# Two graph layers on one core: the score row turned and sent before the first half of the row sums is added up and the second half is fetched

## The chip, the cores and the metric

The kernel runs on one core of a Trainium2 chip. The metric is the time of one execution in microseconds of device time. The kernel before takes 2389.66 us (median of 3 runs, 2389.35 to 2391.8).

The engines are called by the names of the profile: PE is the matrix engine (PEld its weight loads), DVE the vector engine, ACT the scalar engine, POOL the third elementwise engine, SP the engine that here issues nearly every DMA. Each engine works through its own instructions in order; between engines there are semaphores.

## The reference

The input is x (64 samples, 256 nodes, 512 features, float32) and a 256x256 adjacency matrix that all samples share. Two layers follow, each `x = x + layer(relu(layernorm(x)))`.

- Layer 0 is a graph attention with one head: `h = X W` (512 to 256 features), `e[i,j] = leaky_relu(h_i a0 + h_j a1)`, masked by the adjacency, softmax over j, `out = alpha h`, and the result is `[out, h]`, 512 wide again.
- Layer 1 is an attention with 8 heads of 64: q, k, v and the output have 512x512 weights with biases, the scores are masked by the same adjacency, softmax over the keys, and the output projection.

All products are in float32.

## The kernel before, in words

Two samples make a *group* (GB = 2, 512 rows); there are 32 groups (NG). The main loop takes the groups in turn, and each group in two *steps*, one for each sample (b = 0 and b = 1). A step holds the attention heads of layer 1 for sample (g, b), and, threaded between them, pieces of other work: the q, k, v projections of group g+1 (`project`), layer 0 of group g+2 (`first_layer`), the layer norm of the group g+3 (`first_norm`), the output projection of the sample before (`outputs`), and the row sums of this sample's softmax (`fold`). The order is written out by hand: the two strings in `steps` (L1176), one for each step, and an own string for the very first step (L1184). Each letter advances one generator up to its next `yield`: u a product of `project`, s a piece of `first_layer`, o a product of `outputs`, n a piece of `first_norm`, m a mask, f a piece of `fold`. At the start of each step `weigh` of the sample before and then `scores` of the current one are written (the letter S).

The 512x512 products and the first layer's product with W are done by a scheme of seven half-size products (Strassen's, Winograd's form) with sums formed on the elementwise engines. PE's instructions are chained one behind the other in the order in which they are written (`in_order`). On the other engines `not_sooner` ties one instruction behind the engine's last one; where it is not used, the tile framework's scheduler may move an instruction among its neighbours of the same engine.

What the change touches:

- `fold(g, b, p)` (L984): the sums of the masked exponentials. `put` writes a quad of four heads (512 KB) to DRAM ("rows"); `fetch` reads it back in another layout with four DMAs of 128 KB each ("parts", from SP); `add` sums the parts with two instructions on POOL; `sum_up` (L1013) turns a 128x256 block with a DVE transpose and reduces it on DVE into `compact`. The six f's of a step are: put 0 and fetch 0; put 1; add 0; **sum_up 0 and fetch 1**; add 1; sum_up 1 and the reciprocal. The parts of step b = 0 lie in the pool tag "e" with a single buffer, so that fetch 1 may only be issued when sum_up 0 has read the buffer.
- `score_rows(g)` (L621), called in `first_products` (L692) right after the sixth of the seven products of layer 0 is added into H: the layer's attention needs the score of every node along a row. DVE turns eight columns of H (128x32, "rows" from H), SP writes them to DRAM ("line", 2 KB), waits for that to land, and reads the line back broadcast to all 128 partitions ("own", 256 KB).
- `first_layer` (L699) then takes `own`: ACT adds the score of the other node for four blocks (`e<-own,H`), DVE applies the leaky relu (`e<-e`, L758 on), ACT the exponential, DVE the mask, and PE multiplies with H (`po`). The tile e (L748) has the same tag "e" with one buffer, so that ACT's first `e<-own,H` waits for `own` to land **and** for sum_up 1 of the current step to have read the parts.
- `weigh(g, b, p)` (L1038): DVE spreads `compact` into r, PE makes the products `pr`, DVE multiplies both (`oT<-pr,r`), which frees the PSUM banks of pr.
- `scores(g, b)` (L933): PE makes eight score blocks `sc` in four pairs; ACT takes each with an exponential (`p<-sc`), which frees its PSUM bank. In the built program the third pair goes into the banks that `p<-sc` of the first block and `oT<-pr,r` of the first quad set free, and waits for both.

So in the stretch around the change, fetch 1 and the score row's two DMAs stand behind each other on SP, sum_up 0 and the turn of the score row on DVE.

Of the kernel before, what the change touches and what calls it, by code (L numbers as in the profile page):

```python
# [57 lines left out]
def bounded(  # L58
# [24 lines left out]
    vector, scalar, gpsimd, sync = (  # L83
        Remembers(e) for e in (nc.vector, nc.scalar, nc.gpsimd, nc.sync)
    )
# [29 lines left out]
    def after(instruction, name):  # L115

        tc.add_manual_dep(
            instruction.ins, name,
            mybir.DependencyInfo(mybir.DependencyClass.NoSync, mybir.DependencyReason.DATA),
            reason="the engine's order",  # L120
        )

    def not_sooner(engine, operation, *args, **kwargs):

        last = engine.last
        after(getattr(engine, operation)(*args, **kwargs), last)
# [140 lines left out]
        not_sooner(gpsimd, "tensor_sub", t2, w22, w12)  # L267
        not_sooner(gpsimd, "tensor_sub", t4, w21, t2)

    put_last, norm_last, edge_last, sums_last, turn_last, fold_last = [], [], [], [], [], []  # L270

    def last_bias():

# [342 lines left out]
    H = const.tile([P, GT, F1 + 3], F32, name="H")  # L616
# [3 lines left out]

    def score_rows(g):  # L621
        rows = small.tile([P, GT, 8], F32, tag="rows", name=f"rows_{g}", bufs=2)
        last = vector.last
        turned = vector.transpose(rows.rearrange("p t c -> p (t c)"), H[:, :, 0:8])
        for other in [last, *fold_last] if g >= 2 else [last]:
            after(turned, other)
        line = dram.tile([P // 8, S], F32, tag="line", name=f"line_{g}")
        not_sooner(sync, "dma_start", line, rows.rearrange("p t c -> p (t c)")[::8, :])
        own = att.tile([P, P // S, GT, S], F32, tag="r", name=f"own_{g}", bufs=1)
        not_sooner(  # L630
            sync, "dma_start", own.rearrange("p k t j -> p (k t j)"),
            line.rearrange("(o k) j -> o (k j)", o=1).to_broadcast([P, TOK]),
        )
        return own.rearrange("p k t j -> p t k j")
# [209 lines left out]
    def project(g):  # L844
        ops = operands.pop(g)
        parts = {name: projection(g, name, ops) for name in "qkv"}
        for name in "qqkkqqqqqkkkkkvvvvvvv" if g == 0 else "q" * 7 + "k" * 7 + "v" * 7:
            next(parts[name])
            yield
# [78 lines left out]
    def value_differences(g, b):  # L928

        v = qkv["v", g, b][0]  # L930
        not_sooner(gpsimd, "tensor_sub", v[:, 1, :], v[:, 1, :], v[:, 0, :])

    def scores(g, b):  # L933

        (q, q_tag), (k, k_tag) = (qkv[name, g, b] for name in "qk")
        name = f"{g}_{b}"
        p = att.tile([P, NQ * QH, NT, N], F32, tag="p", name=f"p_{name}", bufs=1)
        for i in range(HP):  # L940
            sc = [f"sc_{name}_{2 * i + j}" for j in range(2)]
            sc = [held_bank(2, at) if at.endswith("_3") else mm(at) for at in sc]
            sc = [bank.rearrange("p (k n) -> p k n", k=NT) for bank in sc]
            for kb in range(NT):
                for j in range(2):
                    rows = slice(j * DH, (j + 1) * DH)
                    matmul(
                        sc[j][:, kb, :], k[rows, i, kb * P : (kb + 1) * P], q[rows, i, :],
                        start=True, stop=True,
                    )  # L950
            pair = p[:, 2 * i : 2 * i + 2]
            for j in range(2):
                last = scalar.last
                made = scalar.activation(pair[:, j], sc[j], AF.Exp, scale=scale)
                if g == b == 0:
                    others = [last, *put_last] if i > 1 else [last]
                else:
                    others = [last, *put_last, *norm_last, *edge_last]
                for other in others:
                    after(made, other)  # L960
        places.extend((q_tag, k_tag))
        return p
# [21 lines left out]
    def fold(g, b, p):  # L984

        if g == NG - 1:
            return
        compact = small.tile([P, NQ, N // S], F32, tag="compact", name=f"compact_{g}_{b}", bufs=2)  # L990
        row_sums[g, b] = compact
        pool, tag, bufs = (att, "e", 1) if b == 0 else (big, "hT0", 2)
        rows = []

        def put(quad):
            rows.append(dram.tile([P, QH, N], F32, tag="rows", name=f"rows_{g}_{b}_{quad}"))
            heads = slice(quad * QH, (quad + 1) * QH)
            not_sooner(sync, "dma_start", rows[quad], p[:, heads, 0, :])

        def fetch(quad):  # L1000
            parts = pool.tile([P, P // S, N], F32, tag=tag, name=f"parts_{g}_{b}_{quad}", bufs=bufs)
            for j in range(QH):
                not_sooner(
                    sync, "dma_start", parts[j * S : (j + 1) * S],
                    rows[quad][:, j, :].rearrange("(i a) n -> a i n", a=S),
                )
            return parts

        def add(parts):
            not_sooner(gpsimd, "tensor_add", parts[:, :2], parts[:, :2], parts[:, 2:])  # L1010
            not_sooner(gpsimd, "tensor_add", parts[:, 0], parts[:, 0], parts[:, 1])

        def sum_up(quad, parts):  # L1013
            not_sooner(vector, "transpose", parts[:, 1], parts[:, 0])
            vector.reduce_sum(
                compact[:, quad], parts[:, 1].rearrange("p (k a) -> p k a", a=S), axis=AX.X
            )
            fold_last[:] = [vector.last]

        put(0)  # L1020
        parts = fetch(0)
        yield
        put(1)
        yield
        add(parts)
        yield
        sum_up(0, parts)
        parts = fetch(1)
        yield
        add(parts)  # L1030
        yield
        sum_up(1, parts)
        vector.reciprocal(compact, compact)
        yield
# [138 lines left out]
    additions = (piece for g in range(NG) for piece in residual(g))  # L1173


    steps = ("Smmnfuuuumonmnuofuusssosfsfssuvnofunonfosuo", "Ssmmfusmusmfuososfuosfrsuuonufrounfouunsous")  # L1176
    waiting, late, folds = None, iter(()), iter(())
    for g in range(NG):
        products = project(g + 1) if g + 1 < NG else iter(())
        pieces = first_layer(g + 2) if g + 2 < NG else iter(())  # L1180
        for b, parts in enumerate(steps):
            if g == b == 0:

                parts = "Smmnfuuumnmnuufuussssfsfssuvnfrunnfsuu"  # L1184
            elif g == NG - 1:
                parts = "Smmoomoomooo"
            elif (g, b) == (NG - 2, 1):
                parts += "r"
            if waiting is not None:
                weigh(*waiting)  # L1190
                late = outputs(*waiting[:2])
            i, count = -1, sum(part not in "frv" for part in parts)
            for part in parts:
                i += part not in "frv"
                if part == "u":
                    next(products, None)
                elif part == "o":
                    next(late, None)
                elif part == "s":
                    next(pieces, None)  # L1200
                elif part == "n":
                    next(norms, None)
                elif part == "m":
                    next(masks)
                elif part == "f":
                    next(folds, None)
                    continue
                elif part == "r":
                    next(additions, None)
                    continue  # L1210
                elif part == "v":
                    if g < NG - 1:
                        value_differences(g, b)
                    continue
                else:
                    waiting = (g, b, scores(g, b))
                    masks = mask_pairs(waiting[2], g == NG - 1)
                    folds = fold(*waiting)
                if "v" not in parts and i == (count * 3 // 4, 6)[b] and g < NG - 1:
                    value_differences(g, b)  # L1220
                if i == count // 2:
                    if g == max(NG - 2, 0) and b == 1:
                        conclude()
                    if 0 < g < NG - 3:
                        load(g + 3, b)
                if b == 1 and i == 8 and g >= 2:
                    next(verdict, None)
        run(products)
        run(pieces)
# [373 lines left out]
```

## Time and profile before

| what | value |
|---|---|
| median of 3 runs | 2389.66 us (2389.35 to 2391.8) |
| the profiled execution's own time | 2390.06 us |
| its span in the trace | 2388.3 us |
| PE busy | 2375.2 us, 99% |
| DVE, POOL, ACT busy | 1705.2 us, 1430.5 us, 1023.0 us |
| DMA engines busy | 46.6% (all from SP's queue) |
| turn of the score row, DVE | 30 times, 0.20 us each |
| line, own (DMA) | 30 times, 2 KB and 256 KB |
| parts (DMA) | 496 times 128 KB, four to a fetch |

The page lists each engine's busy time, the chain of work that ended last, the costliest groups of instructions with the idle time before them, and the DMAs with the median time from issue to landing. The timeline lists the instructions of one engine in the order of time: start in us from the beginning of the span, duration, engine, line, operation, out<-in, shapes, and in brackets the idle time before it and what ended it. Nearly all rows say L35 or L137, the lines of the two helpers that record an instruction; so the rows are told apart by their tiles. Matmuls' ends are modelled by the profiler.

### The profile page before, as it was taken

What the parts mean: (1) busy time and instruction counts of PE and PEld (TensorE: products, weight loads), DVE (VectorE), ACT (ScalarE), POOL (GpSimd) and SP (SyncE); (2) the same over time, 40 slices, a digit from 0 to 9 for tenths busy, and PEclk for the clock granted to TensorE, in tenths of its full rate; (3) what the DMA queues carried; (4) which work ended last, traced back from release to release, by engine and by line L of the source; (5) the groups of instructions that cost most, each with busy time, mean ns of one, the idle gap of its engine ahead of it and who ended that gap; (6) DMA issues with size and microseconds to landing.
All of it is one profiled execution on the core that took longest, in us unless ns stands there. A gap on an engine that the chain in (4) does not pass through costs nothing.

```text
span 2388.3 us, 43029 instructions
## 1 busy us (share of the span) xinstructions
PE 2375.2 (99%) x15828; PEld 1993.8 (83%) x15828; DVE 1705.2 (71%) x3345; ACT 1023.0 (43%) x2017; POOL 1430.5 (60%) x1290
## 2 busy tenths in 40 slices
PE   9999999999999999999999999999999999999998
PEld 8888888888888888888888888888888888888886
DVE  7578676686766777767777667776677676777666
ACT  5444444343443444444444434444444444343431
POOL 4565655755657555666656575566665565655552
PEclk9999999999999999999999999999999999999999
DMA  5444445454445544454444455444554445554331
GB/s 185 129 147 146 145 130 163 149 151 143 140 143 155 168 144 137 133 163 149 146 146 140 152 150 161 150 135 139 163 151 146 143 134 161 151 161 141 107 109 46
DMA packets 271864, 343.49 MB, mean 144 GB/s; under 512 B 25376, under 2 KB 217120, under 8 KB 271648
## 3 DMA queue, kind: packets, MB, share of 16 engines
q1 hardware_dynamic: 271648, 340.69, 46.6%
q8 instruction: 126, 2.06, 0.4%
q14 instruction: 90, 0.74, 0.1%
HBM read 176.95 MB, written 163.64 MB: 143 GB/s over the span
## 4 chain that ended last, share of the span: by engine, by line
PE 95%; DVE 2%; ACT 1%; issue 1%; DMA 0%; POOL 0%; SPq 0%; DVEq 0%; ACTq 0%; POOLq 0%
PE pq L137 16%; PE pv L137 16%; PE py L137 16%; PE pk L137 15%; PE sc L137 10%; PE pr L137 9%; PE ph L137 8%; PE po L137 4%; DVE p L35 1%; DMA a_b<-in_L_gnn_a_dram 0%; ACT xn L35 0%; DVE x L35 0%; DVE st L35 0%; ACT e L35 0%; PE total L137 0%
## 5 line engine op out<-in xcount | busy, mean ns | idle before, releaser
L35 POOL TENSOR_TENSOR p<-p 128x512 f32<-128x512 f32 x248 | 393.0, 1598 | 480.9 <-DVE p L35 477.1
L35 ACT ACTIVATE xn<-x,factor 128x512 f32<-128x512 f32 x256 | 194.8, 807 | 412.2 <-POOL factor L35 405.0
L35 DVE TENSOR_TENSOR p<-p,maskT 128x1024 f32<-128x1024 f32 x254 | 347.4, 1389 | 3.2 <-ACT p L35 3.2
L35 DVE TENSOR_TENSOR x<-py,x 128x256 f32<-128x256 f32 x448 | 184.6, 412 | 204.1 <-PE py L137 197.9
L35 ACT ACTIVATE p<-sc 128x512 f32<-128x512 f32 x512 | 257.7, 627 | 94.7 <-PE sc L137 78.3
L35 POOL TENSOR_TENSOR parts<-parts 128x512 f32<-128x512 f32 x248 | 248.1, 1000 | 67.9 <-DMA parts<-rows 54.5
L137 PE MATMUL py<-wo_sb,oT 128*128 128x256 f32 x1024 | 262.4, 379 | 0.6 <-DVE oT L35 0.6
L137 PE MATMUL pk<-hT,wk_sb 128*128 128x256 f32 x1024 | 244.8, 382 | 0.0
L137 PE MATMUL sc<-q,k 64*128 64x256 f32 x2048 | 241.9, 385 | 0.1
L137 PE MATMUL pq<-hT,wq_sb 128*128 128x256 f32 x1024 | 240.1, 382 | 1.1 <-ACT hT L35 0.7
L137 PE MATMUL pv<-wv_sb,hT 128*128 128x256 f32 x1024 | 236.8, 379 | 0.0
L137 PE MATMUL pr<-p,v 128*32 128x256 f32 x4096 | 234.2, 380 | 0.0
L137 PEld LDWEIGHTS sc<-q,k 64*128 64x128 f32 x2048 | 190.8, 187 | 51.8 <-issue 26.3
L35 POOL TENSOR_TENSOR factor<-factor,rexp 128x2 f32<-128x2 f32 (+1 forms) x132 | 117.8, 892 | 178.7 <-DVE factor L35 178.2
L137 PEld LDWEIGHTS pq<-hT,wq_sb 128*128 128x128 f32 x1024 | 191.8, 190 | 36.7 <-issue 10.3
L137 PEld LDWEIGHTS py<-wo_sb,oT 128*128 128x128 f32 x1024 | 194.2, 190 | 28.2 <-DVE oT L35 1.1
L137 PEld LDWEIGHTS pk<-hT,wk_sb 128*128 128x128 f32 x1024 | 189.7, 190 | 33.3 <-issue 9.9
L137 PEld LDWEIGHTS pv<-wv_sb,hT 128*128 128x128 f32 x1024 | 194.6, 190 | 26.5
L137 PEld LDWEIGHTS pr<-p,v 128*32 128x32 f32 x4096 | 126.8, 110 | 97.8 <-issue 18.6
L137 PE MATMUL py<-wo_sb,o_sums 128*128 128x256 f32 x768 | 197.6, 380 | 0.5 <-DVE x L35 0.5
L137 PE MATMUL pv<-wv_sb,sums 128*128 128x256 f32 x768 | 184.2, 383 | 1.9 <-ACT kept_v L35 1.9
L137 PE MATMUL pq<-sums,wq_sb 128*128 128x256 f32 x768 | 181.5, 379 | 0.0
(150 smaller groups left out, 4066.3 us busy)
## 6 DMA issues: line engine op xcount, KB each, us to landing
passed<-xt SPq DMA_DIRECT2D x124, 512.0 KB, 2.9
moved<-passed SPq DMA_DIRECT2D x496, 128.0 KB, 3.5
rows<-p SPq DMA_DIRECT2D x124, 512.0 KB, 3.4
parts<-rows SPq DMA_DIRECT2D x496, 128.0 KB, 3.0
x<-in_x_dram SPq DMA_DIRECT2D x64, 512.0 KB, 4.5
out_dram<-x SPq DMA_DIRECT2D x62, 512.0 KB, 4.0
own<-line SPq DMA_DIRECT2D x30, 256.0 KB, 3.2
wq_sb<-in_L_gnn_Wq_dram SPq DMA_DIRECT2D x2, 512.0 KB, 9.6
```

The costliest lines, as they stand in the source:

```text
L35: instruction = getattr(self.engine, operation)(*args, **kwargs)
L137: in_order(nc.tensor.matmul(*args, **kwargs))
```

## The change

`score_rows` moves ahead of the fourth piece of `fold`. Three edits: in the string of step b = 0, and in that of the first step, the letters `fs` after the fifth s become `sf`, so that the sixth piece of layer 0 (product, sum into H, `score_rows`) is written before sum_up 0 and fetch 1; the list `fold_last`, which held the score row's transpose behind the sum of the row sums, goes; the transpose is tied behind DVE's last instruction alone.

```diff
-    put_last, norm_last, edge_last, sums_last, turn_last, fold_last = [], [], [], [], [], []
+    put_last, norm_last, edge_last, sums_last, turn_last = [], [], [], [], []
...
     def score_rows(g):
         rows = small.tile([P, GT, 8], F32, tag="rows", name=f"rows_{g}", bufs=2)
-        last = vector.last
-        turned = vector.transpose(rows.rearrange("p t c -> p (t c)"), H[:, :, 0:8])
-        for other in [last, *fold_last] if g >= 2 else [last]:
-            after(turned, other)
+        not_sooner(vector, "transpose", rows.rearrange("p t c -> p (t c)"), H[:, :, 0:8])
         line = dram.tile([P // 8, S], F32, tag="line", name=f"line_{g}")
...
         def sum_up(quad, parts):
...
-            fold_last[:] = [vector.last]
...
-    steps = ("Smmnfuuuumonmnuofuusssosfsfssuvnofunonfosuo", "Ssmmfusmusmfuososfuosfrsuuonufrounfouunsous")
+    steps = ("Smmnfuuuumonmnuofuusssosfssfsuvnofunonfosuo", "Ssmmfusmusmfuososfuosfrsuuonufrounfouunsous")
...
-                parts = "Smmnfuuumnmnuufuussssfsfssuvnfrunnfsuu"
+                parts = "Smmnfuuumnmnuufuussssfssfsuvnfrunnfsuu"
```

In the built program the orders of PE, ACT and POOL are the same as before. On SP, in 30 places (once in each group that still has a layer 0 to do), `parts` x4, `line`, `own` becomes `line`, `own`, `parts` x4. On DVE, in the same 30 places, the transpose of the score row goes from behind the transpose and the reduction of the row sums to ahead of them; in 29 of them the sum into H stood ahead of all three already, and in the first one it moves ahead as well. Two other DVE instructions change places with a neighbour, once each.

## The prediction

> **What bounds the kernel now.** I read the page first: engines' busy time and the chain that ended last.
>
> ```profile
> PE 2375.2 (99%) x15828; PEld 1993.8 (83%) x15828; DVE 1705.2 (71%) x3345; ACT 1023.0 (43%) x2017; POOL 1430.5 (60%) x1290
> PE 95%; DVE 2%; ACT 1%; issue 1%; DMA 0%; POOL 0%; SPq 0%; DVEq 0%; ACTq 0%; POOLq 0%
> ```
>
> PE is busy in all but 13 of 2388 us, and its order does not change. So there is little to win anywhere; what the change can do is make PE wait. 0.2% is 4.8 us, about what a measurement of this kernel can tell from no change. I therefore looked for the place where the moved work comes nearest to PE: the timelines of one typical group (around 1207 us; groups come 73.2 us apart and agree to a few hundredths), then the waits of the weight loads. SP and POOL:
>
> ```profile
> 1208.13 1.73 SPq L35 DMA_DIRECT2D parts<-rows  x4
> 1209.90 0.53 SPq L35 DMA_DIRECT2D line<-rows  x1
> 1212.86 0.34 SPq L35 DMA_DIRECT2D own<-line  x1
> 1215.23 0.34 SPq L35 DMA_DIRECT2D passed<-xt  x1
> ...
> 1212.87 2.08 POOL L35 TENSOR_TENSOR parts<-parts 128x512 f32<-128x512 f32 x2
> ```
>
> To be seen: SP stands still from the line's issue to its landing (own follows 0.07 us after it), and POOL adds the fetched parts when its factors are done, at 1212.87; the last part landed at 1212.62. DVE:
>
> ```profile
> 1206.83 0.43 DVE L35 TENSOR_TENSOR H<-ph,kept_h 128x258 f32<-128x258 f32 x1 [0.40 <-PE ph L137]
> 1207.17 0.44 DVE L35 STREAM_TRANSPOSE parts<-parts 128x256 f32<-128x256 f32 x1
> 1207.64 0.42 DVE L35 TENSOR_REDUCE compact<-parts 128x8 f32<-128x256 f32 x1
> 1207.98 0.20 DVE L35 STREAM_TRANSPOSE rows<-H 128x32 f32<-128x32 f32 x1
> ...
> 1216.38 0.42 DVE L35 TENSOR_TENSOR x<-py,x 128x256 f32<-128x256 f32 x1 [0.86 <-PE py L137]
> 1216.72 0.43 DVE L35 STREAM_TRANSPOSE parts<-parts 128x256 f32<-128x256 f32 x1
> 1217.19 0.42 DVE L35 TENSOR_REDUCE compact<-parts 128x8 f32<-128x256 f32 x1
> ...
> 1220.85 1.29 DVE L35 TENSOR_TENSOR oT<-pr,r 128x512 f32<-128x512 f32 x2
> ```
>
> The second parts' transpose does not wait for POOL (done at 1214.95) but for its turn behind `x<-py`. That is the cover of the whole change: 1.77 us. ACT and the weight loads:
>
> ```profile
> 1217.69 1.71 ACT L35 ACTIVATE e<-own,H 128x256 f32<-128x256 f32 x4 [1.28 <-DMA passed<-xt]
> 1221.02 4.03 ACT L35 ACTIVATE p<-sc 128x512 f32<-128x512 f32 x8 [0.24 <-PE sc L137]
> ...
> 1219.86 1.60 PEld L137 LDWEIGHTS sc<-q,k 64*128 64x128 f32 x16 [0.41 <-issue]
> 1221.67 1.60 PEld L137 LDWEIGHTS sc<-q,k 64*128 64x128 f32 x16 [0.22 <-ACT p L35]
> ```
>
> ACT's `e` starts 0.08 us after the reduction's end (1217.61): that frees the tile. The DMA named in brackets is not what it waited for; own had landed at 1216.1. And the loads for the third pair of score blocks already wait: for ACT's first `p<-sc` (ends 1221.62) and DVE's first `oT` (ends 1221.54). This is where the time of PE is decided.
>
> **The change, part by part.** Times are in this group, H's sum ending at 1207.26.
>
> *Turn of the score row first.* One DVE transpose of 0.20 us ahead of 0.86 us; it waits for H (0.03 us in the first group, where it stood right behind it). It ends at 1207.49, the line is issued 0.07 later, as parts were behind their reduction: 1207.56 instead of 1209.90. Sum_up 0 ends 0.3 later, hidden by DVE's idle 1.58 us before `x<-py` at 1210.33; without that cover it would cost its 0.3.
>
> *Own earlier.* Worth nothing: `e` waits for the reduction, and that stays.
>
> *Fetch 1 behind two DMAs and a landing.* What is new on SP ahead of the fetch: the line's landing x, 0.07, own's 0.34 and about 0.13 for the step to the next issue (0.05 between issues, four fulfilled waits of 17 ns). So it starts at 1207.56 + x + 0.54. The trace has no line alone: landing takes 2.5 at least, 2.8 in the median, but always 0.17 after the last part issued ahead of it. Above is thus 2.5; below is 1.7, the 128 KB stores of the output at the end (also SBUF to DRAM). I take 1.9, nearer to those, since the line's packets are done 1.7 to 2.0 after issue even behind the parts. Fetch: 1210.00, 1.87 late.
>
> *The landing of the fetch, T* (first issue to last landing). In these 30 groups 4.28 to 5.46, median 4.43, with only the 2 KB behind it. Now own's 256 KB go ahead and overlap it. Nearest row: the fetches of quad 0 issued behind a 512 KB load that lands about 1.6 us into them: 28 of them, median 4.69 (4.24 to 5.95). I take 4.8, bounds 4.3 and 5.45. Landed: 1214.80.
>
> *POOL's add:* 0.14 after the landing (0.12 to 0.16 where it waited), 2.08 long: 1214.94 to 1217.02. Nothing waits behind it on POOL, which idles 11.2 us afterwards.
>
> *DVE's second transpose:* 0.03 after POOL, 1217.05 instead of 1216.72: 0.33 late. Behind it on DVE stand the reduction, the leaky relu, r and `oT`; ACT's `e` waits for the reduction, and behind `e` on ACT stand the exponentials and all eight `p<-sc`.
>
> *PE:* ACT's path has 0.24 us in hand before `p<-sc`, DVE's only 0.08 (1221.62 less 1221.54). So PE waits s = 0.33 - 0.08 = 0.25 us more in front of the third pair. In general s = x + T - 6.45, and zero below. On SP nothing else is reached: `passed` waits for DVE until 1215.2, the fetch is issued by 1211.7.
>
> *The first group* differs:
>
> ```profile
> 108.10 1.06 PE L137 MATMUL ph<-w_more,hT 128*128 128x129 f32 x8
> ...
> 109.94 0.45 DVE L35 STREAM_TRANSPOSE parts<-parts 128x256 f32<-128x256 f32 x1 [1.14 <-POOL parts L35]
> ...
> 110.91 1.73 SPq L35 DMA_DIRECT2D parts<-rows  x4
> ...
> 117.95 0.40 DVE L35 STREAM_TRANSPOSE parts<-parts 128x256 f32<-128x256 f32 x1
> ```
>
> H's sum, moved ahead of that wait, ends at 109.16 + 0.42 = 109.58; line at 109.88, fetch at 112.32 instead of 110.91, landed 117.12, POOL 117.26 to 119.35, transpose 119.38: 1.43 late. ACT goes from `e` to `p<-sc` without idle time there, and PE's sc already takes 4.37 instead of 3.81 us, so I count 1.4 in full (0.7 to 2.7 with the bounds).
>
> *Sum:* 29 x 0.25 + 1.4 = 8.7 us on the profiled execution's 2390.06. That run is 0.4 above the median of the runs shown, so 2398.4.
>
> [...]
>
> **The rivals.**
>
> *The cover holds (not slower).* One mechanism: fetch 1 still lands in time. It decides at x + T = 6.45 (6.57 for 0.2%). For it: the line with nothing ahead of it may land in 1.7, and the fetch alone needs 4.4: together 6.1. Against it: own's 256 KB in the same DMA engines. Price: s = 0, the first group's 0.7 to 1.2 us alone: 2391, the same within 0.2%.
>
> *The late end (much slower).* x is 2.5 and the fetch, contending with own, takes 5.45: s = 1.5, 29 x 1.5 + 2.7 = 46 us, 2436. For it: landings of 5.3 to 5.5 occur in two groups, and 5.95 behind a load. Against it: medians are 4.4 and 4.7. Halfway (s = 0.9) is 2418.
>
> *A gain.* If the earlier own let `e` start sooner, the loads' present wait (0.22 us, of which PE loses 0.09 in its steps between matmuls) could go: 30 x 0.09 = 2.7 us, 2387, still within 0.2%. Against it: `e` starts behind the reduction, which stands behind `x<-py` as before.
>
> **How the numbers follow.** x + T is 6.7, the bounds 6.0 and 7.95. I give 0.66 to more than 6.57 (slower by over 0.2%; some 0.12 of it to the late end), 0.30 to the cover holding, 0.04 to the gain and anything else, 0.03 of which beyond 0.2%. So faster 0.03, same 0.31, slower 0.66. The likeliest case's own range is 2394 to 2412. The whole range goes from 2390 (cover holds, first group's least price) to 2420 (s = 0.95); the end at 2436 is left out.
>
> **What would show it.** In the changed kernel line is issued about 0.3 us after H's sum, own near 2.3, the first part near 2.7 (before 0.9), the last landing near 7.5 (5.4); POOL's add begins at that landing, not behind its factors; DVE's second transpose waits for POOL, by 0.3 us; the wait of sc's loads grows from 0.2 to near 0.5 us, and the groups come 73.4 instead of 73.2 us apart. Wrong would make it: a line landing below 1.6, a T untouched by own, or another consumer of the late DVE and ACT work that I took to be covered, such as the mask products behind `p<-sc`, 1 us ahead of PE's `po`.

## The result and the profile after

The changed kernel takes 2427.17 us (median of 5 runs, 2424.72 to 2428.97), the kernel before beside it 2389.66 us (5 runs, 2389.35 to 2391.8). The ratio is 1.0154, with an interval of 1.0139 to 1.0169: 37.5 us slower. The direction is the predicted one, the size is not: 8.7 us were predicted, and the end of the range was 2420. The profiled execution of the changed kernel took 2428.97 us, 38.9 more than the profiled one of before; what follows is read from it.

The page's busy times and its chain that ended last:

```profile
PE 2394.3 (99%) x15828; PEld 2011.0 (83%) x15828; DVE 1718.8 (71%) x3345; ACT 1020.3 (42%) x2017; POOL 1429.8 (59%) x1290
PE 78%; DMA 7%; DVE 4%; ACT 3%; POOL 3%; issue 3%; SPq 2%; POOLq 0%; DVEq 0%; ACTq 0%
```

PE is no longer nearly alone on the chain (78%, before 95%): DMA, POOL, DVE and ACT now have shares of it, so something that was covered has come out. PE's busy time grew by 19 us although it has the same instructions; some matmuls follow each other more slowly (in the group below sixteen take 2.26 us instead of 2.00), some run at a granted clock of 0.50 (6.83 us of the first group, 3.41 us of group 14).

A typical group, one 73 us period of the loop. The timelines of SP, POOL, DVE, ACT and the weight loads, with the start in us, the duration, the instructions, and in brackets the idle time before and what ended it:

```profile
1231.37 0.53 SPq L35 DMA_DIRECT2D line<-rows  x1
1233.13 0.35 SPq L35 DMA_DIRECT2D own<-line  x1
1233.78 1.73 SPq L35 DMA_DIRECT2D parts<-rows  x4
...
1239.19 2.08 POOL L35 TENSOR_TENSOR parts<-parts 128x512 f32<-128x512 f32 x2 [2.44 <-DMA parts<-rows]
```
```profile
1230.67 0.43 DVE L35 TENSOR_TENSOR H<-ph,kept_h 128x258 f32<-128x258 f32 x1 [0.40 <-PE ph L137]
1231.13 0.21 DVE L35 STREAM_TRANSPOSE rows<-H 128x32 f32<-128x32 f32 x1
...
1240.22 0.42 DVE L35 TENSOR_TENSOR x<-py,x 128x256 f32<-128x256 f32 x1 [0.86 <-PE py L137]
1241.31 0.45 DVE L35 STREAM_TRANSPOSE parts<-parts 128x256 f32<-128x256 f32 x1 [0.67 <-POOL parts L35]
```
```profile
1242.29 1.71 ACT L35 ACTIVATE e<-own,H 128x256 f32<-128x256 f32 x4 [2.04 <-issue]
...
1245.92 1.86 PEld L137 LDWEIGHTS sc<-q,k 64*128 64x128 f32 x16 [0.62 <-ACT p L35]
```

H's sum ends at 1231.10. The line is issued 0.27 later, lands in 1.69 (own follows 0.07 behind), and fetch 1 starts at 1233.78, 2.68 behind H's sum instead of 0.88. POOL's add begins 0.14 after the last part has landed, so the landing is at 1239.05 and the fetch took 5.27. POOL, which before went straight on from its factors, stands idle for 2.44 us. The second transpose on DVE is no longer in its turn behind `x<-py` (that would be 0.34 after 1240.22, at 1240.56) but waits for POOL: 0.75 late. At the end of this chain the weight loads for the third pair of score blocks wait 0.62 us (before 0.22) and then follow each other more slowly (1.86 for the sixteen instead of 1.60). PE's matmuls of the third and the fourth pair show the wait:

```profile
1245.92 2.26 PE L137 MATMUL sc<-q,k 64*128 64x256 f32 x16 [0.22 <-ACT p L35]
```

The group's 32 score matmuls take 3.81 us before and here 4.48 (2.00, a wait of 0.22, and 2.26): 0.67 lost, 0.08 less than the transpose's delay, as the prediction's formula has it.

Over the whole run, the waits (in total, how often, the longest) of the weight loads and of POOL, in the kernel before:

```profile
PEld sc L137 <- ACT p L35: 7.0, 31, 0.5
```
```profile
POOL parts L35 <- DMA parts<-rows: 54.5, 38, 5.2
```

And in the changed kernel:

```profile
PEld sc L137 <- ACT p L35: 32.7, 30, 3.0
```
```profile
POOL parts L35 <- DMA parts<-rows: 140.7, 63, 5.2
```

Taken from the traces group by group, with "lost" the time by which PE's way from the start of a group's scores to the start of the next group's is longer than before, groups 1 to 29 lost 34.9 us and the first group 4.9, together 39.8. The first group's scores start 0.4 sooner than before, so PE's last matmul comes 39.4 later. In groups 1 to 29 the second transpose is 1.15 late in the mean and the third pair of scores stalls 1.09. Two groups stand out. The first one:

```profile
112.23 1.73 SPq L35 DMA_DIRECT2D parts<-rows  x4
117.78 2.09 POOL L35 TENSOR_TENSOR parts<-parts 128x512 f32<-128x512 f32 x2 [3.73 <-DMA parts<-rows]
...
124.68 4.05 PE L137 MATMUL sc<-q,k 64*128 64x256 f32 x16 [2.58 <-ACT p L35]
128.66 3.12 PE L137 MATMUL pk<-sums,wk_sb 128*128 128x256 f32 x8
```

PE stands idle for 2.58 us, and then its work is slow: sixteen score matmuls take 4.05 us instead of 2.0, eight `pk` 3.12 instead of 1.99. The granted clock says why. In the windows of the trace the columns are the window, its length, the busy time (and instructions) of PE, PEld, DVE, ACT and POOL, the granted clock, the DMA share and GB/s:

```profile
120.74:124.15 3.41, 1.36 (x14) 0.87 (x10) 2.59 (x5) 2.95 (x7) 1.59 (x2) 1.00 0.00 0
124.15:127.56 3.41, 2.88 (x13) 2.88 (x15) 3.29 (x7) 2.71 (x6) 0.00 (x0) 0.50 0.02 5
127.56:130.98 3.42, 3.42 (x12) 2.32 (x10) 3.00 (x4) 1.40 (x3) 1.48 (x1) 0.50 0.00 0
```

For 6.8 us the clock is 0.50. The other is group 14 (near 1172 us), which lost 4.33: its line took 3.62 to land, PE was idle for 2.36 us, and one stretch of 3.4 us ran at 0.50. In the profile of before the clock is 0.5 only at the very end, from 2386.7 us on, when PE's last matmul is 4 us past.

### The profile page after: what moved, and what is told of

The parts are those of the page before. It is cut to its first block, busy times and chain, and to the rows that moved or that the text cites. A ratio compares the mean times of both kernels' runs of the same rounds, so it can differ in the third digit from the quotient of the medians.

```text
span 2427.3 us, 43032 instructions
## 1 busy us (share of the span) xinstructions
PE 2394.3 (99%) x15828; PEld 2011.0 (83%) x15828; DVE 1718.8 (71%) x3345; ACT 1020.3 (42%) x2017; POOL 1429.8 (59%) x1290
## 4 chain that ended last, share of the span: by engine, by line
PE 78%; DMA 7%; DVE 4%; ACT 3%; POOL 3%; issue 3%; SPq 2%; POOLq 0%; DVEq 0%; ACTq 0%
PE pq L137 16%; PE pv L137 16%; PE py L137 12%; PE pk L137 9%; PE sc L137 8%; PE ph L137 7%; PE pr L137 5%; DMA parts<-rows 5%; PE po L137 4%; POOL parts L35 2%; ACT e L35 2%; DMA line<-rows 2%; SPq L35 2%; DVE e L35 1%; DVE p L35 1%
## 5 line engine op out<-in xcount | busy, mean ns | idle before, releaser
L137 PE MATMUL sc<-q,k 64*128 64x256 f32 x2048 | 256.8, 389 | 20.7 <-ACT p L35 20.6
L137 PEld LDWEIGHTS sc<-q,k 64*128 64x128 f32 x2048 | 203.2, 188 | 74.2 <-ACT p L35 32.7
L137 PE MATMUL pk<-sums,wk_sb 128*128 128x256 f32 x768 | 182.7, 381 | 0.0
```

The source lines that it names most:

```text
L137: in_order(nc.tensor.matmul(*args, **kwargs))
```

## The experiments

Theory A: own's 256 KB, issued ahead of fetch 1, are still being moved when the fetch's parts are, and lengthen it; the rest of the loss is the later start. The rival, theory B: the late start alone is the cause, and where the fetch then falls among other work makes it long; own's bytes do not matter. The parts of the change were then done one at a time. The shorthand for all diffs: `score_rows` is cut into `turned_row` (DVE's turn), `sent_row` (line) and `spread_row` (own), without other changes; the diffs are against the changed kernel unless told otherwise.

**Line ahead of the fetch, own behind it.** SP then need not wait for the line's landing before the fetch, and own comes after the parts.

```diff
-        owns[g] = score_rows(g)
+        line = sent_row(g, turned_row(g))
         residual_from(1)
         yield
+        owns[g] = spread_row(g, line)
         product(first, 3, False)
```

> Score row turned and the line sent first, then sum_up 0 and the four DMAs of fetch 1, then own. The fetch no longer waits for the line's landing, and own's 256 KB stand behind it. Theory A (the loss comes from fetch 1 standing behind the line's landing and own, so that POOL's add, DVE's second transpose and ACT's e come late): the fetch starts near 1.1 us after H's sum (before 0.9, after 2.7), lands near 5.6, no group is late, 2390 us within 5. Rival C (the turn of the row ahead of sum_up 0 on DVE, or the line's DMA ahead of the fetch, costs by itself): stays near 2420 or more.

Measured: 2391.05 us, ratio 1.0003 (0.9994 to 1.0013). The fetch starts 1.21 after H's sum and takes 4.35 (median), the transpose is in its turn in every group from 1 to 29, and the wait of the weight loads is back at its old size:

```profile
PEld sc L137 <- ACT p L35: 7.2, 30, 0.9
```

So all but 1.5 of the 37.5 us hang on own, and the wait for the line that it brings, standing ahead of the fetch. The same kernel was run a second time, on another chip:

> The kernel of e1 (line, fetch 1, own) once more, beside the other runs of this call: 2390 to 2391 us, same as before.

Measured: 2391.41 us, 1.0005 (0.9995 to 1.0015), the same again. Its fetch took 4.55 in the median, where the first run's took 4.35: so differences of 0.2 between medians of T are within the spread.

**The wait alone, without own's bytes.** SP reads 64 bytes of the line into a tile that nobody uses, which makes it wait for the line's landing; then come fetch 1, and own behind it.

```diff
+        line = sent_row(g, turned_row(g))
+        probe = small.tile([1, 16], F32, tag="probe", name=f"probe_{g}", bufs=2)
+        not_sooner(sync, "dma_start", probe, line[0:1, :16])
         residual_from(1)
         yield
+        owns[g] = spread_row(g, line)
```

> Line sent first, then a DMA of 64 bytes that reads the line, so that SP waits for its landing as in the changed kernel, then fetch 1, and own last. The fetch starts as late as in the changed kernel (2.7 us after H's sum), but own's 256 KB stand behind it. Theory A (half of the loss is the wait, the other half is the fetch sharing the DMA engines with own ahead of it): first issue to last landing falls from 5.35 to about 4.5, s from about 1.1 to 0.25 in the mean (the late landings of the line keep some), first group near 1.5: 2399 us, 2394 to 2406. Rival B (the fetch takes longer because it runs later, beside other traffic, and not because of own): 5.3 stays, 2420 to 2427.

Measured: 2397.01 us, 1.0032 (1.002 to 1.0045). This is the run that separates the theories: its fetch starts 2.52 after H's sum in the median, nearly as late as in the changed kernel (2.69), but nothing of own is ahead of it. A group of it on SP, POOL and DVE, and the weight loads' wait over the run:

```profile
1283.75 0.53 SPq L35 DMA_DIRECT2D line<-rows  x1
1285.44 0.24 SPq L35 DMA_DIRECT2D probe<-line  x1
1285.97 1.74 SPq L35 DMA_DIRECT2D parts<-rows  x4
...
1290.49 2.08 POOL L35 TENSOR_TENSOR parts<-parts 128x512 f32<-128x512 f32 x2 [1.36 <-DMA parts<-rows]
```
```profile
1292.94 0.44 DVE L35 STREAM_TRANSPOSE parts<-parts 128x256 f32<-128x256 f32 x1
```
```profile
PEld sc L137 <- ACT p L35: 9.6, 32, 1.9
```

The fetch goes from 1285.97 to 1290.35 (POOL's start less 0.14): 4.38, and the median over the groups is 4.36, before 4.44. DVE's transpose has no wait in its brackets here: the cover of 1.77 us just holds. It does not in 11 of the 29 groups, six of them with a line that landed late and the others with a longer fetch; the mean delay is 0.13. The wait for the line costs 7.4 us in all, about 1.4 of it in the first group. The remaining 30 us come with own ahead of the fetch. A start 0.17 later (own's issue takes longer than the 64 bytes') is some 5 of them (29 x 0.17, an estimate from the medians); the rest is the longer fetch and what follows from it. Theory B falls.

**Half of own ahead.** own goes in two DMAs of 64 partitions (128 KB) each, one ahead of fetch 1 and one behind.

```diff
-        owns[g] = score_rows(g)
+        line, own = sent_row(g, turned_row(g))
+        spread_half(line, own, 0)
         residual_from(1)
         yield
+        spread_half(line, own, 1)
```

> The changed kernel with own in two DMAs of 64 partitions (128 KB): one ahead of fetch 1, the other behind it. If the fetch is lengthened by the bytes of own that go ahead of it (none: 4.35 us, 256 KB: 5.35, 256 + 128 KB: 6.5), it takes about 4.85 here; s falls from 1.1 to 0.6 in the mean: 2390 + 29 x 0.6 + 2 = 2409 us, 2404 to 2414. If the presence of a DMA ahead counts and not its bytes: 2422 or more.

Measured: 2415.11 us, 1.0103 (1.0086 to 1.012). The fetch takes 4.80 in the median, halfway between 4.35 and 5.34: what counts is how much goes ahead, and not that a DMA does. Half of the partitions is half of the bytes and half of the packets, so this run does not tell these two apart. The time is 6 us above what was expected; the first group stalls 2.30 and group 14, whose line took 3.63 to land, again falls into a stretch at half clock.

**More bytes ahead.** The changed kernel with a second DMA behind own, which spreads half of the line (128 KB) to a tile that nobody reads.

```diff
+        twin = small.tile([P, TOK // 2], F32, tag="twin", name=f"twin_{g}", bufs=1)
+        not_sooner(
+            sync, "dma_start", twin,
+            line[: P // 16].rearrange("(o k) j -> o (k j)", o=1).to_broadcast([P, TOK // 2]),
+        )
         return own.rearrange("p k t j -> p t k j")
```

> The changed kernel with a second DMA behind own and ahead of the fetch, which spreads half of the line once more over 128 partitions (128 KB, read by nobody). Theory A: the fetch starts 0.4 later (one more issue) and takes about 0.45 longer, so s grows by 0.85 in the mean: 29 x 0.85 on 2427 gives 2452 us, more where PE's idle time passes 2.3 us and its matmuls run at half rate behind it. Rival B (own's traffic does not matter, only the issue): 29 x 0.4, 2439 us.

Measured: 2492.71 us, 1.0436 (1.0418 to 1.0453), well above both. The fetch starts 0.43 later, as expected, but it takes 6.50, that is 1.16 longer than in the changed kernel and not 0.45, and the transpose is 2.74 late in the mean. So theory A has the direction and not the size: with 128 KB each, own's first half cost 0.45, its second 0.54 and the copy 1.16. The packets, the pieces in which the DMA engines move a transfer, fit better. In one group, counted from own's issue to the landing of the fetch in the changed kernel (1233.13 to 1239.04 us) and to shortly before it here (1261.1 to 1268.0):

```profile
DMA packets 721, 0.80 MB, mean 136 GB/s; under 512 B 80, under 2 KB 592, under 8 KB 720
```
```profile
DMA packets 879, 1.00 MB, mean 144 GB/s; under 512 B 96, under 2 KB 736, under 8 KB 877
```
own has 128 packets of 2 KB (720 less 592), so its half 64, and the fetch 512 of 1 KB (592 less 80). The copy of half the line comes in packets of 1 KB, and there are 128 of them (736 less 96, less the fetch's 512), as many as own has. By packets ahead the fetch is longer by 0.45 for 64, 0.99 for 128 and 2.15 for 256: nearly in proportion, which by bytes (128, 256, 384 KB) it is not. No run changed the size of the packets at equal bytes, and own, its half and the copy all read the same 2 KB of DRAM, so that it is the packets is argued and not shown.

Beyond the delay the clock sets in: 13 stretches at half clock within the run, a mean granted clock of 0.991.

**The turn alone.** DVE turns the score row early, as in the change; line and own stay where they were before.

```diff
-        owns[g] = score_rows(g)
+        rows = turned_row(g)
         residual_from(1)
         yield
+        owns[g] = spread_row(g, sent_row(g, rows))
```

> The turn of the score row ahead of sum_up 0 on DVE, as in the changed kernel; SP's order as before (fetch 1, line, own). Theory A: the DVE part is covered, 2390 us within 5. Rival C (DVE's order carries the loss): near 2427.

Measured: 2389.84 us, 1.0001 (0.9991 to 1.001). Sum_up 0 being 0.3 later is free, as predicted.

**The first group as before.** In the string of the very first step the letters are put back; all other groups stay changed.

```diff
-                parts = "Smmnfuuumnmnuufuussssfssfsuvnfrunnfsuu"
+                parts = "Smmnfuuumnmnuufuussssfsfssuvnfrunnfsuu"
```

> The changed kernel, with the letters of the very first step as before; the other 29 groups keep the change. Theory A: the first group's own price goes (4.9 us in the changed kernel's trace: 2.6 us of waiting and the half-rate matmuls behind it), 2427 to 2422.5. Rival (the first group costs as much as any other, near 1.2): 2426.

Measured: 2421.85 us, 1.0141 (1.0126 to 1.0157). The first group is worth 5.3 us (2427.17 less 2421.85) of the 37.5.

**A try at something better.** In the kernel before, sum_up 1 is written one piece sooner, so that `e` on ACT might start sooner and the weight loads' old wait shrink.

```diff
-    steps = ("Smmnfuuuumonmnuofuusssosfsfssuvnofunonfosuo", ...
+    steps = ("Smmnfuuuumonmnuofuusssosfsfssuvnofunofnosuo", ...
```

> The kernel before, with sum_up 1 one piece sooner in step b = 0, so that on DVE it stands ahead of the two transposes of xn and the last output sums. POOL's add is done at 7.7 us after H's sum, so the second transpose starts near 7.8 instead of 9.5, and ACT's e waits for own's landing (8.4 to 9.0) instead: 1 us sooner. If the small wait of the third pair's loads (0.2 us, of which PE loses 0.09) is all that this place costs, 29 x 0.09 = 2.6 us: 2387 us, within 0.2%. If the transposes of xn that come 0.9 us later delay the next norm, no gain or a loss.

Measured: 2392.72 us, 1.0014 (1.0004 to 1.0023), a miss. In the built program the transpose of the parts still stands behind `x<-py`, 9.47 after H's sum as before; only the two transposes of `xn` went behind it, which makes the leaky relu 0.34 later (11.72 instead of 11.38). On PE each group loses about 0.1, and the loads of `pv` wait 11.7 us in all for ACT, where they waited 9.3 before. No version beat the kernel before.

The series in one table (groups 1 to 29 of each profiled execution; start and T, from the first issue to the last landing, are medians, the other two are means; T of the wait-only kernel is worked out from POOL's start; the time is the median of the runs):

| kernel | fetch 1 after H's sum | sent ahead of it | T | transpose late | stall of scores | time, us |
|---|---|---|---|---|---|---|
| before | 0.88 | nothing | 4.44 | 0 | 0 | 2389.66 |
| line ahead, own behind | 1.21 | 2 KB | 4.35 | 0.00 | 0.02 | 2391.05 |
| wait alone | 2.52 | 2 KB, 64 B | 4.36 | 0.13 | 0.10 | 2397.01 |
| half of own ahead | 2.81 | 128 KB, 64 packets | 4.80 | 0.74 | 0.71 | 2415.11 |
| the change | 2.69 | 256 KB, 128 packets | 5.34 | 1.15 | 1.09 | 2427.17 |
| the change and a half | 3.12 | 384 KB, 256 packets | 6.50 | 2.74 | 3.12 | 2492.71 |

## Why the prediction was right in direction and wrong in size

*The mechanism* is the predicted one, link by link: the line goes out 0.27 behind H's sum, SP waits for its landing, fetch 1 lands late, POOL and then DVE's second transpose wait for it, and PE waits for the third pair of scores. The formula s = late - 0.08 holds in the groups where no stretch at half clock follows. The cover on DVE of 1.77 us is real too: the wait-only kernel uses it up and pays little. The mechanism was right, then, and sizes of its terms were not.

*The turn on DVE and the later sum_up 0, counted at nothing*: right (the turn alone, 1.0001).

*The line's landing x, taken as 1.9*: 1.91 in the mean, so the term fits, but as a mean of two cases: 1.67 to 1.72 in some twenty groups and 2.0 to 3.6 in the others. That the mean came out is partly luck: the rows it was taken from did not show these two cases.

*The landing of the fetch, T, taken as 4.8 with bounds of 4.3 and 5.45: the step that failed.* It measured 5.41 in the mean, at its upper bound in the middle of the groups and not now and then. My nearest row was a fetch behind a 512 KB load that lands 1.6 us into it. Here own is issued 0.65 ahead of the first part and takes 3.6 us to land (the page's median), so it lands 2.95 us into the fetch: the overlap is nearly twice as long as in the row I used. The experiments give the size: 0.45 for the first half of own ahead, 0.54 for the second. The packets in the trace show the overlap: in the median of the twenty groups with a line of 1.7, own's packets run until 2.45 us into the fetch, and the fetch's own end 4.49 after its first issue, where they end at 3.51 with own behind. So it is shown that own ahead makes T long, and that the two run at the same time; that the row I used was too short because of its shorter overlap is argued.

*The step on SP from own to the fetch, 0.34 + 0.13 = 0.47*: 0.66 measured in the mean (0.58 to 0.98), 0.2 more. In the typical group above it is 0.35 and then 0.30 to the first part's issue. In that gap the trace has four semaphore instructions on SP. They are shown with 17 to 28 ns each, as I had counted them, but they start 0.05 to 0.07 us after one another (1233.53, 1233.58, 1233.64, 1233.71, then the fetch at 1233.78): here a fulfilled wait took 0.06 us and not 17 ns.

Per group the prediction had 0.25. With T 0.61 longer, the step 0.2 longer and x 0.01 longer it is 1.07, and 1.09 was measured; 29 times that is 31.6 of the 34.9 us lost in these groups. The other 3.3 came behind the stall. In most groups it is 0.08; over the run the loads of `pv` wait 11.5 us for ACT instead of 9.3. In group 14 it is 0.9, where eight `pk` took 3.01 us at half clock instead of 1.99.

*The first group, taken as 1.4 (0.7 to 2.7)*: 4.9 measured, 5.3 by the run with the first step put back. The delay was 2.35 and not 1.43, again mostly by T (5.39), and then the clock doubled the price: 2.58 us of idle PE brought 6.8 us at half clock. Nothing in the sum stood for that: it counted PE's idle time and not what comes behind it.

*The rivals.* That the cover holds was wrong for the change, and nearly right with only the wait ahead of the fetch (2397.01, where it said 2391). A gain did not come: in the typical group `e` still starts 0.08 behind the reduction. The late end (2436) had the right T and the wrong x: with T at its bound and x at the value taken, s is 0.9, and that was the halfway case, priced at 2418. I left it at the edge of the range because I read the two bounds as rare together, where the one alone was enough; the step on SP (29 x 0.2 = 5.8) and the first group (3.5 more) make up the rest to 2427. The chance of 0.12 for the late end was too small for a term that had no direct row.

The stretches at half clock, within the runs 3.41 us long or twice that, came behind windows that mostly had work in them: in the window of that length ahead of the first group's stretch PE had been busy for 1.36 of 3.41 us, and of the 16 stretches within the runs only one followed a window without any work.

## What to carry to other kernels

In these runs a large DMA put ahead of another on the same queue cost the later one more than its issue: 0.45 us for 128 KB in 64 packets, 0.99 for 256 KB in 128, 2.15 for 384 KB in 256. So price it by how long the earlier one stays in flight behind the later one's first issue (own's packets ran until 2.45 us into the fetch), and take a bound, not a middle, where no row has the same overlap. Move the small DMA ahead if it helps, and leave the large one that nobody waits for behind the one that somebody waits for: the same change with own left behind was the same as before (2391.05 us). And where a stall of PE may reach 1.8 us, the shortest that was followed by a stretch at half clock here, count such a stretch behind it as possible (3.41 us at 0.50 behind the 2.36 us of group 14; behind 2.41 us in the kernel with half of own ahead there was none).

## What the runs showed of the hardware that was not expected

**Half clock after partly idle windows.** In the changed kernel and the two with half of own and with a half more ahead there are stretches of granted clock 0.5. In the changed kernel they last 6.83 and 3.41 us and start at 124.15 and 1172.05 us, 1047.89 us or 307 times 3.413 apart. With windows of 3.413 us laid on such starts as a grid, and each window's share of busy PE, a stretch followed a full-clock window whose share was 0.45 or less in all 15 cases within the runs, and none followed a share of 0.49 or more; in between it went either way (0.48 with, 0.47 and 0.48 without). So the same idle time is cheap or dear by where it falls on the grid: group 14's 2.36 us in the changed kernel had a slow stretch behind it, but in the kernel with half of own ahead, 2.41 us of idle time in the first group had no slow stretch behind it (the window had 1.60 of 3.42 us busy):

```profile
120.92:124.34 3.42, 1.60 (x16) 1.08 (x12) 2.65 (x5) 2.89 (x7) 1.65 (x2) 1.00 0.00 0
124.34:127.75 3.41, 2.83 (x19) 2.42 (x20) 3.24 (x8) 3.41 (x9) 0.00 (x0) 1.00 0.02 5
```

In a slow stretch a score matmul that is otherwise shown with 376 ns has 632 ns, and one `pk` follows the other in 0.43 us instead of 0.215.

**A small DMA and the loading of instructions.** The line lands in 1.67 to 1.72 us in some twenty groups and in 2.0 to 3.8 in nine or ten, nearly the same ones in every run that sends it ahead (0, 6, 7, 12, 13, 19, 20, 25, 26, and 14 in three of them). In exactly these a 16 KB packet of an instruction queue started more than 1 us before the line landed. In group 1, and in 14 where the line was not late, one started 0.1 us or less before the landing, and the line took 1.7. The DMA view of the changed kernel, group 14 (from 1154.1 to 1157.8 us):

```profile
q8 instruction: 1, 0.02, 2.2%
...
line<-rows SPq DMA_DIRECT2D x1, 2.0 KB, 3.6
```

In the typical group shown above (1231.37 to 1233.13 us) the view has no such queue and gives the line 1.7 us. That they go together is what the traces show; no run moved the instruction loads, so the cause is not tested.
